# Strassen's products in an attention-and-MLP megakernel: one ScalarE copy out of PSUM with the sums on GpSimd, in place of two VectorE additions; small vectors loaded behind the first weights

## The chip, the cores and the metric

The kernel runs on one core of a Trainium2 chip, in float32 throughout. The metric is the device time of one launch in microseconds: 3781.12 us in the median of three runs (3780.70 to 3781.87).

A core has five engines that run side by side, each through its own queue in order: PE (TensorE, matmuls), DVE (VectorE), ACT (ScalarE), POOL (GpSimd) and SP (SyncE, which here only issues DMAs). They meet in two memories, SBUF and PSUM. Matmuls write PSUM, which has eight banks of 128 x 512 float32.

## The reference

Two layers are applied to x of shape (16, 256, 32, 32): 16 batches, 256 channels, 1024 tokens. Cut to what matters:

```python
# layer 0: attention, 4 heads of 64
qkv  = xs @ w_proj + b_proj
attn = softmax(einsum('bihd,bjhd->bijh', q, k) * 64**-0.5, axis=2)
x    = einsum('bijh,bjhd->bihd', attn, v).reshape(B, S, 256) @ w_out + b_out + xs
# layer 1: attention, 8 heads of 32, then an MLP, each behind a group norm of 32 groups
x = x + attention(group_norm(x, gn1_w, gn1_b), qkv_w, proj_w, proj_b, phys_bias)
h = group_norm(x, gn2_w, gn2_b)
h = gelu(einsum('oc,bchw->bohw', mlp_w1, h) + mlp_b1)          # 256 -> 1024
x = x + einsum('oc,bchw->bohw', mlp_w2, h) + mlp_b2            # 1024 -> 256
```

## The kernel before

**Tiling.** Channels lie on the 128 partitions, in two blocks `co` (0 and 1); the 1024 tokens of a batch lie on the free axis, in two halves `t` of `TB` = 512. So x of one batch is four blocks of 128 x 512, named (co, t), and the result is accumulated in place in the tile of x (three such tiles, `bufs=3`).

**The second MLP matrix by Strassen.** The product of w2 (two output blocks by two halves of the hidden axis) with the hidden activations `g` (two halves of the hidden axis by two halves of the tokens) is a 2 x 2 block product. It is done with Strassen's seven products instead of eight. The seven combinations of w2's quarters are made once at the start, on POOL (`sum_quarters`, L149 to L155). The combinations of `g` are made per batch on POOL, by `combine` (L852 to L858), four additions of 128 x 512 for each of five combinations; for the last batch, 15, they are made on DVE. `mlp` (L828) returns a list of 16 steps `hidden` (first matrix and Gelu) and a list of seven steps `outputs`, one for each product, in the order 2, 5, 3, 4, 1, 6, 7 (the list `products`, L862). A step of `outputs` is a call of `reduce` (L873): four products of 128 x 128 weights with 128 x 512 activations accumulate in a PSUM tile, and then the tile is added to, or subtracted from, the blocks of x that need it. Products 2, 5, 3, 4 and 1 go to two blocks each, products 6 and 7 to one. Each is one DVE instruction from PSUM (L889 with the bias `m2b`, L893 plus, L895 minus). The block whose last contribution this was is sent to memory by a DMA in SP's queue (L897).

**PSUM.** Three tiles of two banks each, "slots" 0 to 2 of the pool `ps_s`, and two single banks of `ps_a`. `wide` (L262) hands out the slot that was handed out longest ago. A step of `outputs` takes one slot, and a unit of scores in the second attention takes all three slots and both single banks. A tile can be written again once the instructions that read it are done.

**Order of the work.** The main loop (L965) goes over the 16 batches. One iteration b runs: the first attention of batch b (`attention_a`), with `later` holding delayed steps; the 16 hidden steps of batch b-1 (L981); the first projections of the second attention; and then the second attention of batch b (`attention_b`), 16 units of scores, each for two blocks of 128 keys. A generator's `yield` marks the end of a unit, and after each unit `run` (L907) inserts one or two other steps, from the dictionary `fill` (L993 to L1015). What is inserted is the rest of this layer's projections, then the seven products of batch b-1, alternating with pairs of projections for the first attention of batch b+1:

```python
for m, at_most in enumerate((1, 4, 6, 8, 10)):
    rest.insert(at_most, first[2 * m + 1 : 2 * m + 3])
```

So in iterations 1 to 14 a unit of scores follows a single product six times (2, 5, 3, 4, 1, 6), and a pair of projections in between. Iteration 0 has no products. In iteration 15 there is no next batch: products 2, 5 and 3 of batch 14 stand three units apart with nothing in between, 4, 1, 6 and 7 follow behind the attention (`end`, L1000), and then come the MLP steps of batch 15 (L1030). A program's order on each engine is the order in which these steps are issued; each engine waits by semaphores for what it needs.

**A unit of the second attention.** PE computes scores into the five PSUM tiles (`s_b`, L497); ACT takes exponentials out of them (`e_b`, L512); DVE sums exponentials (`es_b`, L527); PE weighs the values with the exponentials of the unit before (`acc_b`, L548); DVE adds that to the result (L561). Denominators (L570) are copied out by ACT (L323), travel through memory by SP's DMAs, are inverted by DVE (L332) and come back (L338) for a multiplication on DVE (L595). POOL also adds up the denominators and their inverses (L334, L335).

**Projections.** `qkv` (L725) has steps for q and k (emptied by ACT, L738 or L740) and for v (emptied by ACT, L759, in the first layer and by DVE, L761, in the second). Tiles q0, k0 and v0 of the next batch are made by `qkv_0` (L773).

**The start.** `load_wp` loads the projection weights of q (0), k (1) and v (2), half through ACT's queue and half through POOL's. Those of k are issued first. Then `load_vec` (L110) makes eight small vectors and issues the DMA of each in POOL's queue at once. `at_start` (L169) issues the weights of q and v and builds an identity matrix on POOL, which PE needs to transpose the bias of q and k (`bqk`, L936). `load_rest` (L159) issues the large weights in SP's queue.

Of the kernel before, what the change touches and what calls it, by code (L numbers as in the profile page):

```python
# [8 lines left out]
F32 = mybir.dt.float32  # L9
I32 = mybir.dt.int32  # L10
AF = mybir.ActivationFunctionType
ALU = mybir.AluOpType
AX = mybir.AxisListType

P = 128
GROUPS = 32
EPS = 1e-5
HEADS0, D0 = 4, 64
HEADS1, D1 = 8, 32
TB = 512  # L20
# [34 lines left out]
def kernel(  # L55
# [21 lines left out]
    nc = tc.nc  # L77
    B, C, S = x.shape
    HID = mlp_w1T.shape[1]
    CC = C // P  # L80
    SB = S // P
# [4 lines left out]
    const = ctx.enter_context(tc.tile_pool(name="const", bufs=1))  # L86
# [18 lines left out]
    mhalf = const.tile([P, CC], F32, name="mhalf")  # L105
    nc.gpsimd.memset(mhalf, -0.5)
    ones = const.tile([P, D0 // 2], F32, name="ones")
    nc.gpsimd.memset(ones, 1.0)

    def load_vec(v, n, name):  # L110
        t = const.tile([P, n], F32, name=name)
        nc.gpsimd.dma_start(t, v.rearrange("(c p) -> p c", p=P))
        return t

    bo = load_vec(b_out, CC, "bo")
    g1w = load_vec(gn1_w, CC, "g1w")
    g1b = load_vec(gn1_b, CC, "g1b")
# [4 lines left out]
    m2b = load_vec(mlp_b2, CC, "m2b")  # L122
# [15 lines left out]
    w2s = const.tile([P, 7, HID // P // 2, P], F32, name="w2s")  # L138
# [10 lines left out]
    def sum_quarters():  # L149
        q11, q22 = w2s[:, 2], w2s[:, 3]  # L150
        nc.gpsimd.tensor_sub(w2s[:, 5], w2s[:, 1], q11)
        nc.gpsimd.tensor_add(w2s[:, 1], w2s[:, 1], q22)
        nc.gpsimd.tensor_sub(w2s[:, 6], w2s[:, 4], q22)
        nc.gpsimd.tensor_add(w2s[:, 4], w2s[:, 4], q11)
        nc.gpsimd.tensor_add(w2s[:, 0], q11, q22)  # L155

    def load_rest():  # L159
        nc.scalar.dma_start(pb, phys_bias.partition_broadcast(P))  # L160
        for t, w in weights:
            nc.sync.dma_start(t, w)


    gavg = const.tile([P, P], F32, name="gavg")
# [29 lines left out]
    eones = const.tile([P, HEADS1, D1], F32, name="eones")  # L195
# [3 lines left out]
        nc.vector.tensor_copy(eones, ebias.unsqueeze(2).to_broadcast([P, HEADS1, D1]))  # L199

    bvo = const.tile([P, CC], F32, name="bvo")

    in_range = const.tile([P, 1], I32, name="in_range")

    with ExitStack() as first:
        first_pass(
            first, tc, x, out,
            dict(
                wp=wp, bqk=bqk, pb=pb, bo=bo, g1w=g1w, g1b=g1b, g2w=g2w,
                g2b=g2b, pjb=pjb, m1b=m1b, m2b=m2b, wo=wo, wq=wq, wpj=wpj, w1=w1,  # L210
                w2s=w2s, gavg=gavg, mhalf=mhalf, ones=ones, eones=eones,
                bvo=bvo, at_start=at_start, load_rest=load_rest, exp_bias=exp_bias,
                sum_quarters=sum_quarters,
                in_range=in_range,
            ),
        )
# [14 lines left out]
def first_pass(ctx, tc, x, out, k):  # L231
    nc = tc.nc
    B, C, S = x.shape
    CC, SB, NT = C // P, S // P, S // TB
# [3 lines left out]
    act = ctx.enter_context(tc.tile_pool(name="act", bufs=1))  # L238
# [483 lines left out]
        means()  # L722


    def qkv(key, D, src, weights, b_qk, v_scale, qT, kT, v_dst):  # L725
        def qk(ch, which, t):
            ps = single(f"qk_{key}_{ch}_{which}_{t}")
            for cc in range(CC):
                product(
                    ps,  # L730
                    weights(cc, which)[:, ch * P : (ch + 1) * P],
                    src[:, cc, t * TB : (t + 1) * TB],
                    start=(cc == 0),
                    stop=(cc == CC - 1),
                )
            d = (kT if which else qT)[:, ch, t * TB : (t + 1) * TB]
            if b_qk is None:
                nc.scalar.copy(d, ps)  # L738
            else:
                nc.scalar.activation(  # L740
                    d, ps, AF.Identity, bias=b_qk[:, which, ch : ch + 1]
                )

        def v(n):
            ps = single(f"v_{key}_{n}")
            for i in range(2):
                sb = 2 * n + i
                for cc in range(CC):
                    product(
                        ps[:, i * C : (i + 1) * C],  # L750
                        src[:, cc, sb * P : (sb + 1) * P],
                        weights(cc, 2),
                        start=(cc == 0),
                        stop=(cc == CC - 1),
                    )
            d = v_dst[:, 2 * n : 2 * n + 2]
            ps = ps.rearrange("p (b h d) -> p b h d", b=2, d=D)
            if v_scale is None:
                nc.scalar.copy(d, ps)  # L759
            else:  # L760
                nc.vector.tensor_mul(  # L761
                    d, ps, v_scale.unsqueeze(1).to_broadcast([P, 2, C // D, D])
                )

        return (
            [
                lambda ch=ch, which=which, t=t: qk(ch, which, t)
                for ch in range(CC) for which in (1, 0) for t in range(NT)
            ],
            [lambda n=n: v(n) for n in range(SB // 2)],  # L770
        )

    def qkv_0(b, xb):  # L773
        q = act.tile([P, CC, S], F32, tag="q0", name=f"q0_{b}")
        kk = act.tile([P, CC, S], F32, tag="k0", name=f"k0_{b}")
        v = act.tile([P, SB, HEADS0, D0], F32, tag="v0", name=f"v0_{b}")
        return (q, kk, v), qkv(
            f"a{b}", D0, xb,
            lambda cc, which: k["wp"][:, cc, which].rearrange("p h d -> p (h d)"),
            k["bqk"], None, q, kk, v,  # L780
        )

    def qkv_1(b, xn):
        q = act.tile([P, CC, S], F32, tag="q1", name=f"q1_{b}")
        kk = act.tile([P, CC, S], F32, tag="k1", name=f"k1_{b}")
        v = act.tile([P, SB, HEADS1, D1], F32, tag="v1", name=f"v1_{b}")
        return (q, kk, v), qkv(
            f"b{b}", D1, xn,
            lambda cc, which: k["wq"][:, cc, which * C : (which + 1) * C],
            None, k["eones"], q, kk, v,  # L790
        )

    def attention_0(b, qkv_tiles, xb, norm):
        q, kk, v = qkv_tiles
        stats = small.tile([P, CC, NT, 6], F32, tag="st0", name=f"st0_{b}", bufs=2)

        def project(t, res):
            return out_proj(
                f"o{b}", k["wo"],
                lambda kc: res[:, kc, t * TB : (t + 1) * TB],  # L800
                k["bvo"], xb, t, stats, (lambda: norm(stats)) if t == NT - 1 else None,
            )

        return attention_a(b, q, kk, v, project)

    def attention_1(b, qkv_tiles, xb, norm):
        q, kk, v = qkv_tiles
# [20 lines left out]
    def mlp(b, xb, hn):  # L828
        n4 = HC // 2
        gs = {}  # L830
        add_to = nc.gpsimd if b < B - 1 else nc.vector
# [20 lines left out]
        def combine(to, what, plus):  # L852
# [7 lines left out]


        products = [  # L862
            (2, (0, 0), [(1, 0, True, True), (1, 1, False, False)], ((0, 0), (1, 1))),
            (5, (1, 1), [(0, 1, True, True), (0, 0, False, False)], None),
            (3, (0, 1), [(0, 1, True, False), (1, 1, True, True)], ((0, 1), (0, 0))),
            (4, (1, 0), [(0, 0, True, True), (1, 0, True, False)], ((1, 0), (0, 0))),
            (1, (0, 0), [(0, 0, True, False), (1, 1, True, False)], None),
            (6, (0, 1), [(1, 1, True, False)], None),
            (7, (1, 0), [(0, 0, True, False)], None),
        ]  # L870
        missing = {(0, 0): 4, (0, 1): 2, (1, 0): 2, (1, 1): 4}

        def reduce(number, right, outs, then):  # L873
            ps = wide(f"m2_{b}_{number}")[:, 0, :]
            for i in range(n4):
                product(
                    ps, k["w2s"][:, number - 1, i], gs[(*right, i)],
                    start=(i == 0), stop=(i == n4 - 1),
                )
            for co, t, plus, bias in outs:  # L880
                missing[co, t] -= 1

                num = 2 if b == B - 1 and number == 7 else 1
                for u in range(num):
                    n = TB // num
                    sl = slice(t * TB + u * n, t * TB + (u + 1) * n)
                    y, p = xb[:, co, sl], ps[:, u * n : (u + 1) * n]
                    if bias:
                        nc.vector.scalar_tensor_tensor(  # L889
                            y, p, k["m2b"][:, co : co + 1], y, ALU.add, ALU.add  # L890
                        )
                    elif plus:
                        nc.vector.tensor_add(y, y, p)  # L893
                    else:
                        nc.vector.tensor_sub(y, y, p)  # L895
                    if not missing[co, t]:
                        nc.sync.dma_start(out[b, co * P : (co + 1) * P, sl], y)  # L897
            if then:
                combine(*then, True)
# [35 lines left out]
    ps, n = bank("bqk", 0), brow.shape[0]  # L935
# [399 lines left out]
```

## Time and profile before

| What | Value |
|---|---|
| Median of three runs | 3781.12 us (3780.70 to 3781.87) |
| Profiled execution, time and span | 3782.21 us, 3780.4 us |
| Mean granted TensorE clock | 0.998 |
| PE busy | 3751.6 us (99%) |
| DVE busy | 2459.8 us (65%) |
| ACT busy | 2036.6 us (54%) |
| POOL busy | 565.4 us (15%) |
| From one iteration to the next, iterations 1 to 14 | 233.45 us |
| First scores of the first attention | 34.08 us after the span's start |
| Score unit behind a product, from its start to that of acc_b: products 2, 5, 3, 4, 1, 6 | 2.65, 3.30, 3.17, 2.65, 2.64, 1.90 us |
| Additions of g on POOL (L855) | 300 of 1553 ns in the mean |

A line of the timeline gives the start, the time it took, the engine, the source line, the operation, what it writes and reads, the shape and the number of instructions; in brackets stands the idle time of the engine before it, and what ended it. A line of the waits gives who waited, for whom, the sum in us, how often, and the longest. The times of PE come from modelled ends, so a stretch of PE is best measured from the start of one group to the start of the next.

### The profile page before, as it was taken

To read this page: it belongs to the slowest core of one execution; us is meant where nothing else is said; L and a number is where in the kernel's file an instruction comes from. 1 tells how busy PE (TensorE), PEld (TensorE's weight loads), DVE (VectorE), ACT (ScalarE), POOL (GpSimd) and SP (SyncE) were. 2 spreads that over 40 slices of the span, in tenths; PEclk is the share of its full clock that TensorE was granted. 3 is DMA by queue.
4 is the path that set the end of the run, shared out by engine and by line. 5 is a ranking of instruction groups with operands and counts; after the bars stand their busy time and mean duration, and the time that the engine had idled before them with its cause. 6 is when DMAs were issued, how large, how long until landed. Compare 5 with 4: busy or idle time off the path is not lost.

```text
span 3780.4 us, 79539 instructions
## 1 busy us (share of the span) xinstructions
PE 3751.6 (99%) x34349; PEld 1329.2 (35%) x34349; DVE 2459.8 (65%) x2850; ACT 2036.6 (54%) x2624; POOL 565.4 (15%) x550
## 2 busy tenths in 40 slices
PE   9999999999999999999999999999999999999998
PEld 3333342333423334233342333333333333333323
DVE  4685657756576665766657666576665766657675
ACT  4565546555465554545546455554555546555462
POOL 1002112021120211202012020120201212011111
PEclk9999999999999999999999999999999999999999
DMA  2000100001001000010000101001010000100000
GB/s 85 10 16 10 33 12 13 30 10 33 12 13 35 7 30 13 19 30 7 30 13 19 29 7 34 9 19 30 8 34 7 23 25 13 30 7 23 14 8 26
DMA packets 63396, 77.80 MB, mean 21 GB/s; under 512 B 35038, under 2 KB 37854, under 8 KB 63038
## 3 DMA queue, kind: packets, MB, share of 16 engines
q1 hardware_dynamic: 60892, 71.85, 6.4%
q8 instruction: 271, 4.44, 0.5%
q10 hardware_dynamic: 1746, 0.40, 0.1%
q14 instruction: 87, 0.71, 0.1%
q0 software_dynamic: 400, 0.41, 0.1%
HBM read 54.28 MB, written 17.56 MB: 19 GB/s over the span
## 4 chain that ended last, share of the span: by engine, by line
PE 90%; DVE 4%; issue 3%; DMA 1%; ACT 1%; SPq 0%; POOL 0%; DVEq 0%; ACTq 0%; POOLq 0%
PE s_b L497 12%; PE m L836 12%; PE s_a L363 12%; PE acc_b L548 11%; PE acc_a L384 11%; PE m L309 7%; PE qk_b L309 6%; PE qk_a L309 5%; PE v_b L309 3%; PE o L309 3%; PE v_a L309 3%; PE j L309 3%; DVE es_b L527 2%; PE den_b L570 1%; PE den_a L415 1%
## 5 line engine op out<-in xcount | busy, mean ns | idle before, releaser
L512 ACT ACTIVATE e_b<-s_b 128x1024 f32<-128x1024 f32 (+1 forms) x1280 | 983.0, 864 | 394.2 <-PE s_b L497 394.2
L527 DVE TENSOR_TENSOR es_b<-es_b,e_b 128x1024 f32<-128x1024 f32 x768 | 961.5, 1300 | 258.2 <-ACT e_b L512 256.5
L371 ACT ACTIVATE e_a<-s_a 128x1024 f32<-128x1024 f32 x512 | 521.4, 1025 | 359.7 <-PE s_a L363 348.5
L497 PE MATMUL s_b<-q,k 32*64 32x512 f32 x8192 | 588.9, 603 | 14.9 <-DVE x L895 6.8
L855 POOL TENSOR_TENSOR g<-g,g 128x512 f32<-128x512 f32 x300 | 458.8, 1553 | 760.4 <-PE m L309 739.7
L363 PE MATMUL s_a<-q,k 64*64 64x512 f32 x4096 | 532.5, 593 | 1.1
L384 PE MATMUL acc_a<-e_a,v 64*64 64x512 f32 x4096 | 528.4, 589 | 0.0
L396 DVE TENSOR_TENSOR es_a<-es_a,e_a 128x1024 f32<-128x1024 f32 x384 | 469.3, 1222 | 74.7 <-ACT e_a L371 59.1
L548 PE MATMUL acc_b<-e_b,v 128*32 128x512 f32 x4096 | 494.6, 601 | 0.0
L836 PE MATMUL m<-gn_h,w 128*128 128x512 f32 x1024 | 452.8, 596 | 0.0
L309 PE MATMUL m<-g,w2s 128*32 128x512 f32 (+1 forms) x3320 | 404.2, 592 | 0.0
L844 ACT ACTIVATE g<-m,m1b 128x512 f32<-128x512 f32 x256 | 174.4, 687 | 288.7 <-PE m L836 288.5
L497 PEld LDWEIGHTS s_b<-q,k 32*64 32x64 f32 x8192 | 174.4, 130 | 395.5 <-issue 198.1
L836 PEld LDWEIGHTS m<-gn_h,w 128*128 128x128 f32 x1024 | 191.0, 190 | 235.9 <-issue 232.4
L384 PEld LDWEIGHTS acc_a<-e_a,v 64*64 64x64 f32 x4096 | 161.8, 133 | 277.7 <-issue 235.9
L363 PEld LDWEIGHTS s_a<-q,k 64*64 64x64 f32 x4096 | 152.4, 133 | 278.3 <-issue 208.0
L561 DVE TENSOR_TENSOR res_b<-res_b,acc_b 128x512 f32<-128x512 f32 x192 | 131.2, 683 | 181.6 <-PE acc_b L548 181.6
L309 PE MATMUL qk_a<-x,wp 128*32 128x512 f32 (+1 forms) x1856 | 236.1, 594 | 3.4 <-DMA wp<-in_L_conv_w_proj_dram 3.4
L548 PEld LDWEIGHTS acc_b<-e_b,v 128*32 128x32 f32 x4096 | 108.8, 109 | 359.4 <-ACT e_b L512 195.3
L309 PE MATMUL qk_b<-gn_g,wq 128*32 128x512 f32 (+1 forms) x1280 | 234.1, 592 | 0.0
L309 PEld LDWEIGHTS m<-g,w2s 128*32 128x32 f32 (+1 forms) x3320 | 122.2, 112 | 261.5 <-issue 246.6
L761 DVE TENSOR_TENSOR v<-v_b,eones 128x512 f32<-128x512 f32 x64 | 44.1, 688 | 201.8 <-PE v_b L309 201.8
(130 smaller groups left out, 2436.4 us busy)
## 6 DMA issues: line engine op xcount, KB each, us to landing
d_a<-row_a SPq DMA_DIRECT2D x64, 256.0 KB
rd_b<-row_b SPq DMA_DIRECT2D x252, 64.0 KB
out_dram<-x SPq DMA_DIRECT2D x63, 256.0 KB
x<-in_x_dram SPq DMA_DIRECT2D x30, 512.0 KB
x<-in_x_dram SPq DMA_DIRECT2D x4, 256.0 KB
w<-in_L_conv_mlp_w_dram SPq DMA_DIRECT2D x1, 1024.0 KB
w2s<-in_L_conv_mlp_w_dram SPq DMA_DIRECT2D x4, 256.0 KB
sp_b<-rd_b SPq DMA_DIRECT2D x63, 8.0 KB
```

Source lines behind the costliest of these rows:

```text
L309: nc.tensor.matmul(o[sl], w[:, sl], r, **flags)
L363: nc.tensor.matmul(s[h : h + HALF, g, :], kT[g * D : (g + 1) * D, c, kb * P + h : kb * P + h + HALF], qT[g * D : (g + 1) * D, c, t * TB : ...
L371: nc.scalar.activation(e, s, AF.Exp, scale=float(D) ** -0.5)
L384: nc.tensor.matmul(accs[i][h][g * D : (g + 1) * D, :], v[h * HALF : (h + 1) * HALF, kb, c * 2 + g], e[h * HALF : (h + 1) * HALF, g, :], st ...
L396: nc.vector.tensor_add(sums[i], held[i] if kb == 1 else sums[i], e)
L497: nc.tensor.matmul(outs[g][h : h + HALF, :], kT[g * D : (g + 1) * D, c, k0 : k0 + HALF], qT[g * D : (g + 1) * D, c, t * TB : (t + 1) * TB] ...
L512: nc.scalar.activation(to, s, AF.Exp, scale=float(D) ** -0.5)
L527: ins = nc.vector.tensor_add(d, es[n] if kb == 0 else d, es[2 * block + n])
L548: nc.tensor.matmul(acc[g * D : (g + 1) * D, :], v[:, kb + m, c * G + g], es[2 * m + g // 2][:, g % 2, :], start=(m == 0), stop=(m == 1),)
L836: nc.tensor.matmul(ps, k["w1"][:, cc, hc * P : (hc + 1) * P], hn[0][:, cc, t * TB : (t + 1) * TB], start=(cc == 0), stop=(cc == CC - 1),)
L844: nc.scalar.activation(g, ps, AF.Gelu, bias=k["m1b"][:, hc : hc + 1])
L855: ins = (add_to.tensor_add if plus else add_to.tensor_sub)(d, d, gs[(*what, i)])
```

## The change

Two parts.

First, the vectors. `load_vec` no longer issues its DMA; it puts it on a list, and `load_rest` issues the eight DMAs in POOL's queue, behind the weights of q and v and behind the identity matrix.

Second, the products. A product that goes to two blocks is read from PSUM by one ACT instruction into a quarter of an SBUF tile `lent`, 128 x 4 x 512, which takes the place of the next batch's v0 (so v0 is now made only when its first step runs). The two additions then read `lent` instead of PSUM, on POOL for batches 0 to 14 and on DVE for batch 15. Products 6 and 7 stay on DVE, from PSUM. The bias m2b goes in with the ACT instruction of products 2 and 5. Each of these is added to one block and subtracted from another, so the second block would miss two biases' worth; products 6 and 7 add twice m2b (`m2b2`) there. `combine` behind products 2, 3 and 4 stands behind the two additions in POOL's queue. The matmuls and SP's DMAs keep their order.

```diff
     def load_vec(v, n, name):
         t = const.tile([P, n], F32, name=name)
-        nc.gpsimd.dma_start(t, v.rearrange("(c p) -> p c", p=P))
+        vectors.append((t, v.rearrange("(c p) -> p c", p=P)))
         return t
...
         nc.gpsimd.tensor_add(w2s[:, 0], q11, q22)
+        nc.gpsimd.tensor_add(m2b2, m2b, m2b)
...
         for t, w in weights:
             nc.sync.dma_start(t, w)
+        for t, v in vectors:
+            nc.gpsimd.dma_start(t, v)
...
-            d = v_dst[:, 2 * n : 2 * n + 2]
+            d = v_dst()[:, 2 * n : 2 * n + 2]
...
-        v = act.tile([P, SB, HEADS0, D0], F32, tag="v0", name=f"v0_{b}")
+        made = []
+        def v():
+            if not made:
+                made.append(act.tile([P, SB, HEADS0, D0], F32, tag="v0", name=f"v0_{b}"))
+            return made[0]
...
-            for co, t, plus, bias in outs:
+            bias, num, add_to = None, 1, nc.vector
+            if len(outs) == 1:
+                bias = k["m2b2"]
+                num = 2 if b == B - 1 and number == 7 else 1
+            elif number in (2, 5):
+                bias = k["m2b"]
+            co = outs[0][0]
+            if len(outs) == 2:
+                if not lent:
+                    lent.append(act.tile([P, 4, TB], F32, tag="v0", name=f"lent_{b}"))
+                m = lent[0][:, number % 4]
+                if bias is not None:
+                    nc.scalar.activation(m, ps, AF.Identity, bias=bias[:, co : co + 1])
+                    bias = None
+                else:
+                    nc.scalar.copy(m, ps)
+                ps = m
+                if b < B - 1:
+                    add_to = nc.gpsimd
+            for co, t, plus in outs:
                 missing[co, t] -= 1
-                num = 2 if b == B - 1 and number == 7 else 1
+                n = TB // num
                 for u in range(num):
-                    n = TB // num
                     sl = slice(t * TB + u * n, t * TB + (u + 1) * n)
                     y, p = xb[:, co, sl], ps[:, u * n : (u + 1) * n]
-                    if bias:
+                    if bias is not None:
                         nc.vector.scalar_tensor_tensor(
-                            y, p, k["m2b"][:, co : co + 1], y, ALU.add, ALU.add
+                            y, p, bias[:, co : co + 1], y, ALU.add, ALU.add
                         )
-                    elif plus:
-                        nc.vector.tensor_add(y, y, p)
                     else:
-                        nc.vector.tensor_sub(y, y, p)
+                        (add_to.tensor_add if plus else add_to.tensor_sub)(y, y, p)
                     if not missing[co, t]:
                         nc.sync.dma_start(out[b, co * P : (co + 1) * P, sl], y)
```

## The prediction

> **What bounds the kernel now.** I read the page first. Its line for PE says 99% busy, so what PE does not idle away visibly must be found elsewhere. Then who waited for whom, PE only: barely 20 us in all.
>
> ```profile
> PE   3751.6 (99%) x34349; PEld 1329.2 (35%) x34349; DVE 2459.8 (65%) x2850; ACT 2036.6 (54%) x2624; POOL 565.4 (15%) x550
> ...
> PE s_b L497 <- DVE x L895: 6.8, 16, 1.7
> PE s_b L497 <- DVE res_b L561: 4.3, 5, 1.8
> PE qk_a L309 <- DMA wp<-in_L_conv_w_proj_dram: 3.4, 1, 3.4
> PE s_b L497 <- DVE x L889: 2.9, 14, 0.2
> ```
>
> Lines 889 and 895 are the second of the two VectorE additions that empty a Strassen product: scores wait for its PSUM. The page warns that ends of matmuls are modelled, so I took the third view, the timeline of PE, and measured from the start of one group to the start of the next (iteration 3, counted from 0, second attention):
>
> ```profile
> 829.32 2.72 PE L497 MATMUL s_b<-q,k 32*64 32x512 f32 x32
> 831.97 1.92 PE L548 MATMUL acc_b<-e_b,v 128*32 128x512 f32 x16
> 833.71 3.62 PE L309 MATMUL qk_a<-x,wp 128*32 128x512 f32 x32
> 837.26 1.97 PE L497 MATMUL s_b<-q,k 32*64 32x512 f32 x32
> 839.16 1.92 PE L548 MATMUL acc_b<-e_b,v 128*32 128x512 f32 x16
> 840.90 3.62 PE L309 MATMUL m<-g,w2s 128*32 128x512 f32 x32
> 844.45 1.95 PE L497 MATMUL s_b<-q,k 32*64 32x512 f32 x24
> 846.73 1.09 PE L497 MATMUL s_b<-q,k 32*64 32x512 f32 x8 [0.34 <-DVE x L895]
> 847.74 1.92 PE L548 MATMUL acc_b<-e_b,v 128*32 128x512 f32 x16
> ```
>
> The same 32 score matmuls take 837.26 to 839.16 = 1.90 us after a projection (qk_a) and 844.45 to 847.74 = 3.29 us after product 5. Only 0.34 of these 1.39 us is shown as a wait; the rest hides in overlapping modelled ends, as after product 2 (829.32 to 831.97 = 2.65). The cause stands on DVE and ACT:
>
> ```profile
> 837.39 0.69 ACT L740 ACTIVATE q<-qk_a,bqk 128x512 f32<-128x512 f32 x1 [1.03 <-PE qk_a L309]
> ...
> 845.24 0.75 DVE L889 SCALAR_TENSOR_TENSOR x<-m,m2b,x 128x512 f32<-128x512 f32 x1
> 845.90 0.68 DVE L895 TENSOR_TENSOR x<-x,m 128x512 f32<-128x512 f32 x1
> ```
>
> A unit of scores uses all three two-bank slots, the one last filled as its third, needed 0.9 us in. One ACT operation frees that slot 837.39+0.69-837.26 = 0.82 us after the scores begin, with no loss. Two DVE operations free it at 1.49 us when DVE is free (product 2: the second ends at 830.81, the scores began at 829.32), and at 845.90+0.68-844.45 = 2.13 us after product 5, where a normalising multiply stands ahead. Iterations 1 to 14 repeat these numbers to 0.01 us: 2.65, 3.30, 3.17, 2.65, 2.64 after products 2, 5, 3, 4, 1 and 1.90 after product 6, which has a single DVE addition.
>
> The start is the other loss:
>
> ```profile
> 7.46 0.73 POOL L112 DMA_DIRECT2D m2b<-in_L_conv_mlp_b_dram  x1
> ...
> 8.25 1.53 POOL L93 DMA_DIRECT2D wp<-in_L_conv_w_proj_dram  x2
> ...
> 15.12 12.12 PE L309 MATMUL qk_a<-x,wp 128*128 128x512 f32 x22 [3.43 <-DMA wp<-in_L_conv_w_proj_dram]
> ```
>
> The query weights stand in POOL's queue behind eight vectors. After the 3.43 us wait the window 15 to 20 us shows a granted clock of 0.50.
>
> **What the Trainium skill says.** "PSUM — Partial Sum Buffer", The four PSUM rules: GpSimd cannot touch PSUM, so the ACT copy is what lets POOL add at all. "SBUF — State Buffer", Who interferes with whom: a VectorE instruction with two SBUF inputs contends with a GpSimd instruction that reads SBUF; PE and ACT wait on nobody. The trace agrees: the sum of exponentials (L527) takes 1.22 us with POOL idle and 1.74 us in the mean (1.53 to 2.31) where POOL adds throughout. "ScalarE: Activation LUTs", Table sets: identity and copy are in every set; here L740 (Identity) runs among exponentials and the only loads are one per change between Exp and Gelu (31). "TensorE: Matmul & The Clock Gate", part 1: an idle window of about 3.4 us halves the clock; the 0.50 above agrees.
>
> **The change, part by part, against the span of 3780.4 us** (profiled execution 3782.21, median 3781.12; the median is 0.7 above the span).
>
> *Vectors behind the weights.* POOL loses 8 issues of 0.73 to 0.91 us (2.33 to 8.19) ahead of the two wp issues, which so start near 2.5 instead of 8.25. The first wp of that queue, issued at 1.30, landed at 6.80; the last two landed 1.9 and 1.2 us after their predecessors, so I estimate 8 to 9.5 us. PE needs them at about 11.1 and 20. The identity matrix on POOL (10.07 to 10.36) moves to about 5, so the 0.27 us of waiting for it goes too. From 10.16, PE then has 0.1 us of transpose, 24 matmuls at 0.429 us (the spacing of the 64 hidden matmuls, 27.47/64) and 6.84 us of v projections: scores begin at 27.4 instead of 34.08. **-6.6 us.** Bounds: -3.7 (the clock drops anyway) to -7. Behind the moved vectors on POOL stand the sums of w2 quarters, which start when w2s lands (20.13), while the vectors are issued by about 11; m2b2, one tiny addition, hides there. bo is read near 30 us, the others after 90; their DMAs took 3.6 to 5.7 us. x's second half shares the DMA engines with 256 KB more and is needed only near 13.7.
>
> *Products 2, 5, 3, 4, 1 of batches 0 to 13 (iterations 1 to 14).* Removed from DVE: two operations each, 7.0 us per batch. Added on ACT: one of 0.69 (Identity with bias, row L740) or 0.59 (copy, row L759), placed where ACT idles: before product 5's exponentials it waited 3.35 us for PE, and they begin at 845.57, 1.12 us after the scores do, while the copy ends at 0.82. So the projection case applies: 1.90. Saved per iteration 0.75+1.40+1.27+0.75+0.74 = 4.91, times 14 = **-68.7 us**. If ACT were not free the copy would cost what it removes.
>
> *Added on POOL:* ten additions per batch, SBUF to SBUF, price of row L855: 1.27 alone, 1.59 beside DVE, so 15.9 us. POOL is busy 22.6 of the 74.8 us from 825.8 to 900.6. Combining g after products 2, 3 and 4 moves behind two additions (3.2 us): 3.2+6.7 = 9.9 us after product 3, with about 19 us to product 4. DVE gains 7.0 and loses by contention 15.9 x (1.74-1.22)/1.74 = 4.8; it was busy 55.3 of those 74.8. The accumulator addition (L561) that frees PE's bank has some 2 us in hand, so I take 0; bounds 0 to +0.2 us for each of 70 products (+14), and no gain below 0, since 1.90 is the floor of every unit. The tile lent takes v's place: v's first eviction comes at about 893.6, the last POOL addition ends near 888.5. Output DMAs in SP's queue wait for POOL: product 3's goes from 854.4 to 855.4, and the next issue behind it is at 859.7.
>
> *Products 6 and 7* add 2 x m2b: 0.75 instead of 0.69 us on DVE. Slot freed at 0.88 instead of 0.82; where v_b is emptied by a late 0.69 us operation the trace has 1.97. +0.07 x 14 = **+1.0**.
>
> *Iteration 15* (products 2, 5, 3 of batch 14, other units without filling): product 2's 4.66 us, and the half clock behind it (acc_b 3.15, den_b 1.26), shrink until ACT binds: exponentials end at 3648.36, then the denominator copy, so the next scores start near 3649.1 instead of 3652.47, -3.4. After products 5 and 3 the exponentials ran back to back (3.83 for 5), so ACT paces and little comes: -0.2. POOL's longer queue after product 3 stretches DVE: +0.6. **-3**, bounds -7 and +1.
>
> *End:* product 7's two half additions carry a bias, +0.1. Products 4 and 1 put four additions into POOL before the power for the last norm (3718.81): about +0.2. Batch 15's additions stay on DVE, behind a copy, under 24 us of matmuls. **+0.3.**
>
> Sum: -6.6-68.7+1.0-3.0+0.3 = -77.0; span 3703.4, predicted 3704.1.
>
> **Rivals.** (1) *Contention gives back a third to a half*: POOL's additions slow DVE so that L561 is late. For: single pairs of L527 took 4.5 us beside POOL. Against: the 2 us in hand. 0.4 us per product is 70 x 0.4 = 28: 3732. (2) *The change doesn't free the scores*, because something else holds them at the same moment: only the start is left, 3774. Against: the 1.90 after projections and product 6. (3) *Slower*: product 6 adds on DVE to a block that product 1's POOL addition must have finished; DVE stands there in order, with L527 and L561 behind it. POOL has about 12 us in hand (888.5 against 900.7). From product 2's end (829.4) POOL has 22 operations before that block is ready; it comes too late once they take (900.7-829.4)/22 = 3.2 us each, and the iteration loses more than its 4.8 us gain from 3.5 us on. At 3.6 us it loses 22 x 0.4 = 8.8: 3781 + 14 x (8.8-4.8) - 9 = 3828. The longest L855 seen is 2.29, the mean beside DVE 1.59.
>
> **How the numbers follow.** Forecast 0.72 (its own range 3694 to 3718: start ±2, contention 0 to 14, iteration 15 ±4), rival 1 0.17 (3718 to 3755), rival 2 0.05 (3755 to 3774), no change 0.02, rival 3 0.03; 0.01 is a gain beyond the forecast. Eight in ten: 3693 to 3724, the upper end into rival 1. 0.2% (7.6 us) is about what a measurement of this kernel tells from no change: faster 0.95, same 0.02, slower 0.03.
>
> **What would show it.** PE's waits on x L889/L895 gone; 32 scores after every product 1.90; iterations 228.6 us apart instead of 233.45; no wait for wp, scores from 27.4 us; L527's mean up from 1300 to 1350 to 1420 ns; POOL some 810 us busy. I am wrong if scores stay over 2.5 us after a product, if L561 or POOL appears as PE's releaser in iterations 1 to 14, or if DVE waits for POOL's x.

## The result, and the profile after

The changed kernel takes **3763.81 us** in the median (3763.14 to 3765.74, five runs) against 3781.12 of the kernel before beside it (five runs). The ratio is 0.9954, with a 95% interval of 0.9940 to 0.9969. It is faster, but by 17.3 us where 77 were forecast.

The profiled spans go from 3780.4 to 3762.0 us, 18.4 less. I split both at the first hidden-layer matmul of the MLP of batch 0, and at the same place 14 iterations on:

| Part | Before | After | Difference | Forecast |
|---|---|---|---|---|
| Start, up to the first hidden matmul | 287.10 | 280.58 | -6.5 | -6.6 |
| Iterations 1 to 14, each | 233.45 | 232.15 | -1.30, 14 times -18.2 | -4.84, 14 times -67.7 |
| Iteration 15 and the end | 224.99 | 231.30 | +6.3 | -2.7 |

The start came as forecast. The page's line of busy times and the waits of PE show what took the place of the old waits:

```profile
PE 3699.7 (98%) x34349; PEld 1327.1 (35%) x34349; DVE 2563.5 (68%) x2700; ACT 2085.8 (55%) x2704; POOL 904.7 (24%) x701
```

```profile
PE s_b L502 <- DVE res_b L566: 47.0, 48, 3.1
PE gm_h L314 <- DVE mean_c_h L689: 3.4, 1, 3.4
```

The waits of scores for the additions to x (formerly L889 and L895) are gone. In their place stand 47.0 us of waiting for L566, the addition of a unit's result to the accumulator (L561 before), which frees one of the two single banks. VectorE has 150 instructions fewer and is busy 104 us longer.

The timeline of PE, iteration 3, around products 5, 3 and 1 (start, duration, line, what it writes and reads, and in brackets the idle time and what ended it):

```profile
831.04 3.62 PE L314 MATMUL m<-g,w2s 128*32 128x512 f32 x32
835.40 1.98 PE L502 MATMUL s_b<-q,k 32*64 32x512 f32 x32 [0.75 <-DVE res_b L566]
837.31 1.92 PE L553 MATMUL acc_b<-e_b,v 128*32 128x512 f32 x16
839.05 3.62 PE L314 MATMUL m<-g,w2s 128*32 128x512 f32 x32
843.32 1.98 PE L502 MATMUL s_b<-q,k 32*64 32x512 f32 x32 [0.65 <-DVE res_b L566]
...
869.39 3.62 PE L314 MATMUL m<-g,w2s 128*32 128x512 f32 x32
874.40 1.98 PE L502 MATMUL s_b<-q,k 32*64 32x512 f32 x32 [1.39 <-DVE res_b L566]
876.30 1.92 PE L553 MATMUL acc_b<-e_b,v 128*32 128x512 f32 x16
```

From the start of the scores to acc_b it is 835.40 to 837.31 = 1.91 us after product 5 (3.30 before), and 1.90 after product 1 (2.64 before): this is what the change was forecast to do. But products 5, 3 and 1, ahead of them, now last 4.36, 4.27 and 5.01 us from start to start, where a product without a wait lasts 3.55: 0.81 + 0.72 + 1.46 = 3.0 us lost per iteration. Another 0.46 us go behind product 1's unit: from its acc_b to the next scores it is 6.62 us, where it was 6.16 before. Of the 4.75 us that the six units of scores gained, 1.3 are left.

Why L566 is late can be read on VectorE and GpSimd, at the same time:

```profile
822.44 8.92 DVE L532 TENSOR_TENSOR es_b<-es_b,e_b 128x1024 f32<-128x1024 f32 x4 [3.44 <-ACT e_b L517]
...
831.45 3.30 DVE L532 TENSOR_TENSOR es_b<-es_b,e_b 128x1024 f32<-128x1024 f32 x2
834.67 0.67 DVE L566 TENSOR_TENSOR res_b<-res_b,acc_b 128x512 f32<-128x512 f32 x1
```

```profile
821.11 2.51 POOL L929 TENSOR_TENSOR x<-x,lent 128x512 f32<-128x512 f32 x2 [1.24 <-ACT lent L911]
823.58 8.93 POOL L868 TENSOR_TENSOR g<-g,g 128x512 f32<-128x512 f32 x4
```

From 823.58 on the two engines run side by side and both crawl: four sums of exponentials in 8.92 us, four additions of g in 8.93, 2.23 us each. Alone, a pair of such sums takes 2.35 us (1.22 for one), and two additions took 2.51 us at 821.11. So beside additions a sum takes nearly as long as a sum and an addition one after the other. L566, one of whose inputs is in PSUM, takes its usual 0.67 us; it is only late. The groups say it for the whole run (busy time and mean in ns, then idle time before). First the kernel before, then the changed one:

```profile
L527 DVE TENSOR_TENSOR es_b<-es_b,e_b 128x1024 f32<-128x1024 f32 x768 | 961.5, 1300 | 258.2 <-ACT e_b L512 256.5
L855 POOL TENSOR_TENSOR g<-g,g 128x512 f32<-128x512 f32 x300 | 458.8, 1553 | 760.4 <-PE m L309 739.7
```

```profile
L532 DVE TENSOR_TENSOR es_b<-es_b,e_b 128x1024 f32<-128x1024 f32 x768 | 1100.7, 1480 | 249.5 <-ACT e_b L517 249.4
L868 POOL TENSOR_TENSOR g<-g,g 128x512 f32<-128x512 f32 x300 | 514.1, 1738 | 20.8 <-ACT g L857 20.8
L929 POOL TENSOR_TENSOR x<-x,lent 128x512 f32<-128x512 f32 x150 | 268.7, 1811 | 152.6 <-ACT lent L914 96.0 <-ACT lent L911 56.5
```

The sums' mean rose from 1300 to 1480 ns (1350 to 1420 forecast), that of the old additions of g from 1553 to 1738.

At the end of the kernel, VectorE, GpSimd and PE in one stretch of the timeline:

```profile
3686.13 3.70 POOL L868 TENSOR_TENSOR g<-g,g 128x512 f32<-128x512 f32 x3
3689.79 0.19 POOL L590 TENSOR_TENSOR isum<-isum,part 128x1 f32<-128x1 f32 x1
...
3690.01 0.17 DVE L1070 TENSOR_REDUCE top<-isum 128x1 f32<-128x16 f32 x1 [3.03 <-POOL isum L590]
...
3694.12 0.38 PE L314 MATMUL gm_h<-mean_c_h,gavg 128*128 128x2 f32 x2 [3.38 <-DVE mean_c_h L689]
```

VectorE's range check of the denominators (L1070) waits 3.03 us for a tiny GpSimd sum, which now stands behind the two additions and three of the four combinations of product 4. Behind the check on VectorE wait the last projection's eviction and the norm's statistics, and PE waits 3.38 us for these. In the kernel before it waited 0.5 us at this place:

```profile
PE gm_h L309 <- DVE mean_c_h L684: 0.5, 1, 0.5
```

In the changed kernel, the clock granted behind this wait, from 3694.2 to 3700, is 0.71.

### The profile page after: what moved, and what is told of

It is laid out like the page before. It is cut to its first block, busy times and chain, and to the rows that moved or that the text cites. A ratio compares the mean times of both kernels' runs of the same rounds, so it can differ in the third digit from the quotient of the medians.

```text
span 3762.0 us, 79474 instructions
## 1 busy us (share of the span) xinstructions
PE 3699.7 (98%) x34349; PEld 1327.1 (35%) x34349; DVE 2563.5 (68%) x2700; ACT 2085.8 (55%) x2704; POOL 904.7 (24%) x701
## 4 chain that ended last, share of the span: by engine, by line
PE 85%; issue 7%; DVE 5%; DMA 2%; ACT 1%; SPq 0%; ACTq 0%; POOL 0%; DVEq 0%
PE m L849 12%; PE s_a L368 12%; PE acc_a L389 11%; PE s_b L502 11%; PE acc_b L553 9%; PE m L314 6%; PE qk_b L314 6%; PE qk_a L314 4%; PE v_a L314 3%; PE v_b L314 3%; PE o L314 3%; PE j L314 3%; DVE es_b L532 3%; PE den_b L575 1%; DMA rd_b<-row_b 1%
## 5 line engine op out<-in xcount | busy, mean ns | idle before, releaser
L532 DVE TENSOR_TENSOR es_b<-es_b,e_b 128x1024 f32<-128x1024 f32 x768 | 1100.7, 1480 | 249.5 <-ACT e_b L517 249.4
L376 ACT ACTIVATE e_a<-s_a 128x1024 f32<-128x1024 f32 x512 | 521.0, 1024 | 360.1 <-PE s_a L368 348.4
L502 PE MATMUL s_b<-q,k 32*64 32x512 f32 x8192 | 530.1, 604 | 47.9 <-DVE res_b L566 47.0
L868 POOL TENSOR_TENSOR g<-g,g 128x512 f32<-128x512 f32 x300 | 514.1, 1738 | 20.8 <-ACT g L857 20.8
L339 POOL TENSOR_TENSOR dsum<-dsum,sp_b 128x16 f32<-128x16 f32 x63 | 45.0, 715 | 1150.5 <-DMA sp_b<-rd_b 1150.5
L929 POOL TENSOR_TENSOR x<-x,lent 128x512 f32<-128x512 f32 x150 | 268.7, 1811 | 152.6 <-ACT lent L914 96.0
L502 PEld LDWEIGHTS s_b<-q,k 32*64 32x64 f32 x8192 | 164.7, 131 | 381.3 <-issue 166.3
```

The costliest lines, as they stand in the source:

```text
L376: nc.scalar.activation(e, s, AF.Exp, scale=float(D) ** -0.5)
L502: nc.tensor.matmul(outs[g][h : h + HALF, :], kT[g * D : (g + 1) * D, c, k0 : k0 + HALF], qT[g * D : (g + 1) * D, c, t * TB : (t + 1) * TB] ...
L532: ins = nc.vector.tensor_add(d, es[n] if kb == 0 else d, es[2 * block + n])
L868: ins = (add_to.tensor_add if plus else add_to.tensor_sub)(d, d, gs[(*what, i)])
L929: (add_to.tensor_add if plus else add_to.tensor_sub)(y, y, p)
```

## The experiments

All are compared with runs of the kernel before on the same chip (3780.8 to 3781.4 us in the median). "Period" is the time from one iteration to the next, iterations 1 to 14; "the rest" is iteration 15 and the end. Line numbers after an edit can be shifted by a few from those of the changed kernel. The main question is the first table's middle row: do the 3.5 us per iteration that are missing come from contention between GpSimd and VectorE, or from something else in the new way of the products?

**The parts alone.** First the kernel before with the vectors moved; then the changed kernel with the vectors loaded at once:

```diff
     def load_vec(v, n, name):
         t = const.tile([P, n], F32, name=name)
-        vectors.append((t, v.rearrange("(c p) -> p c", p=P)))
+        nc.gpsimd.dma_start(t, v.rearrange("(c p) -> p c", p=P))
```

> The kernel before with only the vectors loaded behind the weights. If the two parts of the change add up: 3781.1 - 6.5 = 3774.6 us, scores from 27.6 us on, iterations still 233.45 us apart. If the start's gain is partly due to the second part: over 3776.

> The changed kernel with the vectors loaded at once as before. If the parts add up: 3763.8 + 6.5 = 3770.3 us, iterations 232.15 us apart. If they do not add up: away from that by over 2 us.

Vectors alone: 3774.55 us, ratio 0.9982 (0.9975 to 0.9989), period 233.45, first scores at 27.19 us instead of 34.08. Products alone: 3770.06 us, ratio 0.9971 (0.9960 to 0.9981), period 232.16. The gains of 6.8 and 11.3 us add up to 18.1; both together gave 17.3. The difference of 0.8 us is less than the runs of one kernel differ, so nothing shows that the parts disturb each other, and the shortfall is in the products.

**The additions on VectorE, still behind the ACT copy.** GpSimd keeps the combining of g:

```diff
                     nc.scalar.copy(m, ps)
                 ps = m
-                if b < B - 1:
-                    add_to = nc.gpsimd
```

> The changed kernel with the two additions of each product on VectorE for all batches, from the SBUF copy that ScalarE makes. Theory A (what the freed PSUM slots gained, 4.8 us per iteration, was given back because additions on GpSimd and sums of exponentials on VectorE exclude each other, and the accumulator addition then comes late): scores 1.90 us after each product, no waits of PE for L566 in iterations 1 to 14, iterations 228.6 us apart, 3703 to 3708 us. Rival B (VectorE has too much in front of the accumulator addition as soon as units follow each other faster, whoever adds): waits for L566 stay, iterations 231 us or more, 3740 us or more. Rival C (ScalarE's copy itself delays): same as B, with ScalarE as releaser.

Measured 3727.03 us, ratio 0.9858 (0.9842 to 0.9875), period 230.26, the rest 221.45: 36.8 us better than the change, and between the two expectations. The ACT copy is thus not what costs. PE's only stall in an iteration is 1.53 us, after the projections that follow product 4. VectorE and GpSimd behind product 4:

```profile
853.70 2.94 DVE L927 TENSOR_TENSOR x<-x,lent 128x512 f32<-128x512 f32 x2 [0.91 <-ACT lent L914]
856.55 4.53 DVE L532 TENSOR_TENSOR es_b<-es_b,e_b 128x1024 f32<-128x1024 f32 x2
861.00 0.67 DVE L566 TENSOR_TENSOR res_b<-res_b,acc_b 128x512 f32<-128x512 f32 x1
...
853.11 6.89 POOL L868 TENSOR_TENSOR g<-g,g 128x512 f32<-128x512 f32 x4
```

The combining, which was there before, now meets additions of VectorE from SBUF (2.94 us for two; the two from PSUM took 0.75 and 0.68) and then two sums (2.27 each). Even work that was not moved has become dearer.

This kernel tells one thing more. Nothing stands ahead of the combining in GpSimd's queue here, so behind product 2 it begins as early as in the kernel before, 1.2 us after the product's first matmul:

```profile
812.59 3.62 PE L314 MATMUL m<-g,w2s 128*32 128x512 f32 x32
...
813.80 5.19 POOL L868 TENSOR_TENSOR g<-g,g 128x512 f32<-128x512 f32 x3 [39.32 <-PE m L314]
```

And the sums of exponentials (L532) last 1318 ns in the mean over the whole run, close to the 1300 of the kernel before and far from the 1480 of the changed one.

**GpSimd writes but does not add.** Each GpSimd addition is replaced by a one-column copy and two fills of the block, so the result lacks these products:

```diff
+                    elif add_to is nc.gpsimd:
+                        nc.gpsimd.tensor_copy(y[:, :1], p[:, :1])
+                        for _ in range(2):
+                            nc.gpsimd.memset(y, 0.0)
```

> The changed kernel in which GpSimd does not add (the contribution of products 2, 5, 3, 4 and 1 is left out for batches 0 to 14): for each addition it reads one column of the copy and then fills the block twice with zeros, about 1.2 us of GpSimd that reads nothing from SBUF but that column. Theory A in its narrow form (what excludes VectorE is GpSimd's reading): sums of exponentials beside these fills take 1.22 us, the mean of L532 falls from 1480 to below 1300 ns, iterations 228.6 us apart, about 3705 us. Rival D (any GpSimd work on SBUF beside VectorE, or a late GpSimd queue, costs the same): mean 1400 or more, iterations 231 to 232 us, about 3760 us.

A single run took 3708.76 us, with a period of 229.07. The mean of the sums is 1348 ns, above the 1300 expected, and the trace shows why:

```profile
829.26 1.77 POOL L929 COPY x<-lent 128x1 f32<-128x1 f32 x2 [2.83 <-ACT lent L911]
830.96 1.92 POOL L931 MEMSET x<- 128x512 f32 x4
...
838.54 6.96 POOL L868 TENSOR_TENSOR g<-g,g 128x512 f32<-128x512 f32 x4
...
830.90 2.35 DVE L532 TENSOR_TENSOR es_b<-es_b,e_b 128x1024 f32<-128x1024 f32 x2
...
840.06 4.32 DVE L532 TENSOR_TENSOR es_b<-e_b,e_b 128x1024 f32<-128x1024 f32 x2
```

The four fills run wholly beside a pair of sums, and the pair keeps its 2.35 us. Beside the combining, 8 us later, a pair takes 4.32. Even the tiny copies take turns: 1.77 us for two while VectorE ends a sum and a multiplication, 0.30 where VectorE is idle (836.41). In this run, GpSimd instructions that only write cost VectorE nothing; those that read do.

**Nothing on GpSimd behind the products.** The third experiment, with the combining behind products 2, 3 and 4 on VectorE too:

```diff
-                ins = (add_to.tensor_add if plus else add_to.tensor_sub)(
+                on = nc.vector if plus else add_to
+                ins = (on.tensor_add if plus else on.tensor_sub)(
```

> The kernel with the additions of the products on VectorE (the run before this one), in which the sums of g behind products 2, 3 and 4 go to VectorE too, so that GpSimd adds nothing during the second attention. Theory A (GpSimd and VectorE exclude each other): L532 falls to 1.22 us in the mean, the wait for L566 of 1.5 us per iteration behind product 4 goes, iterations 228.5 to 229.5 us apart, 3700 to 3712 us. Rival B (VectorE has too much to do in order): its 2.6 us bursts in front of the accumulator addition bring waits for L566 after products 2, 3 and 4, iterations over 230.3 us, slower than 3727 us.

Measured **3704.41 us** (3702.49 to 3705.03), ratio 0.9799 (0.9782 to 0.9815), period 228.82, the rest 216.26. It beats both kernels. VectorE has 22 more instructions per iteration than in the changed kernel, and its sums, and PE's waits for L566, are:

```profile
L532 DVE TENSOR_TENSOR es_b<-es_b,e_b 128x1024 f32<-128x1024 f32 x768 | 899.7, 1219 | 199.4 <-ACT e_b L517 198.6
```

```profile
PE s_b L502 <- DVE res_b L566: 6.2, 7, 2.6
```

**GpSimd's instructions cut in halves.** If the engines take turns, instruction by instruction, a sum should wait for half as much when each GpSimd addition covers 256 columns:

```diff
-                        (add_to.tensor_add if plus else add_to.tensor_sub)(y, y, p)
+                        for h in range(0, TB, TB // 2):
+                            c = slice(h, h + TB // 2)
+                            (add_to.tensor_add if plus else add_to.tensor_sub)(
+                                y[:, c], y[:, c], p[:, c]
+                            )
```

and the same in `combine`.

> The changed kernel with every addition of GpSimd beside the second attention (to x, and of g) cut into two of 256 columns: the same work in twice as many instructions. Theory A as turn-taking (a VectorE sum waits out one GpSimd instruction, 1.07 us, and then runs): a sum beside GpSimd takes about 1.75 us in place of 2.29, the waits for L566 (2.8 us per iteration) shrink by half or more, 3735 to 3752 us. If VectorE loses by the amount of GpSimd work and not by turns: 2.29 stays in sum over more instructions, no gain or a loss by GpSimd's added overhead, 3760 to 3785 us.

Measured 3730.28 us, ratio 0.9866 (0.9850 to 0.9883), period 229.87, the rest 229.7: better than expected. Wholly beside GpSimd, a sum lasts 1.75 us in the median, not 2.29. Above 1.22 that is 0.53 instead of 1.07: half. The work is the same; only the length of a turn differs. The waits for L566 in iterations 1 to 14 are gone. The price is on GpSimd, whose pairs of halves now take longer than one whole, and a new wait of ACT comes of it:

```profile
871.67 4.75 POOL L933 TENSOR_TENSOR x<-x,lent 128x256 f32<-128x256 f32 x4
...
876.46 0.59 ACT L765 COPY v<-v_a 128x512 f32<-128x512 f32 x1 [2.33 <-POOL x L933]
```

The first copy of v waits until product 1's additions are done with the lent tile, whose memory it takes: the unit of scores behind it lasts 3.09 us instead of 1.90. The prediction named this memory and had 5 us in hand for it; with halves it is used up.

**Batch 14 on VectorE.** The changed kernel with `b < B - 2` in place of `b < B - 1`, for the last row of the first table:

> The changed kernel with the additions of batch 14, whose products run in iteration 15 and behind it, on VectorE. If the last stretch is 6.1 us longer since VectorE's range check stands in front of the last norm and waits for GpSimd's sum of inverses, which stands behind product 4's additions: 3763.8 - 6 = 3758 us, and no wait of 3.4 us for mean_c_h. If something else lengthened it: 3763 us.

Measured 3754.8 us, ratio 0.9931 (0.9915 to 0.9948); period 232.15 as in the changed kernel, the rest 221.46 instead of 231.30. Of these 9.8 us, 3.1 are in iteration 15's attention and 6.7 behind it; PE's wait for mean_c_h is not there. So the loss at the end comes from batch 14's additions on GpSimd; that it runs through the sum of inverses is read from the waits above.

**The combining moved in the kernel before.** Is the gain of the fifth kernel that of moving the combining alone? The same edit in `combine`, made in the kernel before, whose products still leave PSUM by two VectorE additions:

> The kernel before, with one edit: the combining of g behind products 2, 3 and 4 is done by VectorE instead of GpSimd. The products still leave PSUM by two VectorE additions, and the vectors are loaded as before. It tells whether the gain of moving the combining (22.6 us from the third to the fifth kernel of the experiments) is there on its own. Theory: no. The third score slot is still freed by two VectorE operations, so the 4.9 us per iteration stay, and VectorE gets 12 operations of 0.68 us more against about 4 us less stretching; 3775 to 3800 us, period 233 to 234.5. Rival, that contention alone set the time and the ScalarE copy is not needed: about 3758 us or less, period 231.9 or less.

Measured 3767.83 us, ratio 0.9963 (0.9949 to 0.9977), period 232.93. It gains 13.6 us, which I had not expected, but far less than the rival said. Only about half of it comes from the 14 iterations (0.5 us each); iteration 15 and the end take 217.3 us instead of 225.0. Score units after products 2, 5, 3, 4, 1 last 2.65, 3.30, 2.65, 2.65, 2.64 us: only product 3's has changed (3.17 before). The third slot is still freed late, as here behind product 5:

```profile
844.07 1.95 PE L497 MATMUL s_b<-q,k 32*64 32x512 f32 x24
846.35 1.09 PE L497 MATMUL s_b<-q,k 32*64 32x512 f32 x8 [0.34 <-DVE x L896]
847.37 1.92 PE L548 MATMUL acc_b<-e_b,v 128*32 128x512 f32 x16
...
844.87 0.74 DVE L890 SCALAR_TENSOR_TENSOR x<-m,m2b,x 128x512 f32<-128x512 f32 x1
845.53 0.68 DVE L896 TENSOR_TENSOR x<-x,m 128x512 f32<-128x512 f32 x1
```

The ACT copy is needed for the slots. To use nearly all that it gives, the combining has to leave GpSimd; halves used a good part of it with the combining left there.

**The change's own GpSimd additions, without the combining.** The changed kernel with that same edit in `combine` and nothing else:

> The changed kernel with the combining behind products 2, 3 and 4 on VectorE, while GpSimd keeps the ten additions per iteration that the change gives it. Theory, a price of 1.07 us of VectorE per GpSimd addition wherever it comes from: VectorE is busy about as long as in the changed kernel, but behind products 3 and 4 it is late by 2 x 1.07 + 4 x 0.68 = 4.9 us instead of 6 x 1.07 = 6.4, so that the waits for the accumulator addition shrink without going: 3712 to 3740 us, sums of exponentials 1280 to 1350 ns in the mean. Rival, that only the long runs of combining on GpSimd hurt and the change's own additions are free: 3704 us as with all additions on VectorE, and the sums at 1220 to 1250 ns.

Measured **3705.76 us** (3705.11 to 3707.84), ratio 0.9801 (0.9785 to 0.9817), period 228.80. The time is the rival's, and cannot be told from that of the fifth kernel: my theory of one price for every addition fell. In the profiled executions the iterations are equal, and the rest is 219.44 us, 3.2 more than in the fifth kernel. The rival is right on the time, but not on its reason. GpSimd's additions are not free. VectorE beside GpSimd behind product 3:

```profile
834.50 2.35 DVE L532 TENSOR_TENSOR es_b<-es_b,e_b 128x1024 f32<-128x1024 f32 x2
836.77 4.66 DVE L869 TENSOR_TENSOR g<-g,g 128x512 f32<-128x512 f32 x4
841.35 0.68 DVE L566 TENSOR_TENSOR res_b<-res_b,acc_b 128x512 f32<-128x512 f32 x1
...
836.40 3.27 POOL L930 TENSOR_TENSOR x<-x,lent 128x512 f32<-128x512 f32 x2 [4.64 <-ACT lent L915]
```

Two GpSimd additions meet four short VectorE additions, which take 4.66 us instead of 2.49; two turns are lost, and then it is over. L566 ends at about 842.0, and PE wants its bank only at 843.58.

The busy time of VectorE from product 2 to the scores behind product 6 gives the price of a GpSimd addition in each kernel. VectorE's own work is taken from the two kernels that have none on GpSimd there: 58.07 us with the ACT copy (in it, five pairs of additions to x at 1.29 us and three times four of g at 2.49, which the others give to GpSimd in whole or in part), 58.40 without it (with three times 2.49).

| Kernel | GpSimd additions | VectorE busy | its own | lost | per addition |
|---|---|---|---|---|---|
| Before | 12 of g | 55.35 | 58.40 - 7.5 = 50.9 | 4.4 | 0.37 |
| Changed | 12 of g, 10 to x | 62.66 | 58.07 - 7.5 - 6.4 = 44.2 | 18.5 | 0.84 |
| Additions on VectorE | 12 of g | 61.10 | 58.07 - 7.5 = 50.6 | 10.5 | 0.88 |
| Only additions on GpSimd | 10 to x | 58.21 | 58.07 - 6.4 = 51.7 | 6.5 | 0.65 |
| In halves | 24 and 20 halves | 55.69 | 44.2 | 11.5 | 0.52 a pair |

A full turn costs 1.07 us. How near an addition comes to it depends on what VectorE does at that moment. In the kernel with the additions on VectorE (0.88), half of the 10.5 us lies on these additions themselves: the ten are busy for 11.54 us, against 6.47 in the fifth kernel. In the kernel before they read PSUM and kept their time.

## Why the prediction was right and wrong

**Right: the start.** -6.5 for -6.6 us. The weights landed at 7.07 and 7.66 us, before the 8 to 9.5 that I estimated, scores began at 27.58 instead of 27.4.

**Right: the slots.** The units of scores behind the five two-block products last 1.90 or 1.91 us in all 14 iterations, as forecast from the unit behind a projection. The unit behind product 6 lasts 2.03, 0.13 more for the 0.07 forecast. The copy is on ACT in time. The last experiment, with the combining off GpSimd, has the forecast's period (228.80 us for 228.6) and no stall of PE in an iteration. That its span of 3703.7 us also meets the 3703.4 of the sum is in part luck: the start, the iterations and the rest gained 6.1, 65.1 and 5.5 us where 6.6, 67.7 and 2.7 were forecast.

**Wrong: the step "loses by contention 15.9 x (1.74-1.22)/1.74 = 4.8", and from it "I take 0" for L561.** Contention rose by 14.1 us per iteration (18.5 - 4.4 in the table), three times as much, and VectorE's busy time in the stretch did not fall by 2.2 but rose by 7.3 us. Two things were wrong in that step. The mean of 1.74 is too low for a sum that meets additions from its start to its end: in the changed kernel such a sum lasts 2.29 = 1.22 + 1.07 us, and in the kernel before the 45 sums that lie wholly inside a run of GpSimd additions have a median of 2.30 already. And I priced only the ten new additions, leaving the twelve old ones at what they cost before, 0.37. (The ten also took GpSimd 1.81 us each, not 1.59.) Here is why the old ones were cheap, from the timeline of the kernel before, product 2, whose matmuls begin at 825.77:

```profile
826.99 4.73 POOL L855 TENSOR_TENSOR g<-g,g 128x512 f32<-128x512 f32 x3 [39.32 <-PE m L309]
...
825.77 2.35 DVE L527 TENSOR_TENSOR es_b<-e_b,e_b 128x1024 f32<-128x1024 f32 x2
829.46 0.75 DVE L889 SCALAR_TENSOR_TENSOR x<-m,m2b,x 128x512 f32<-128x512 f32 x1 [1.33 <-PE m L309]
830.13 0.68 DVE L895 TENSOR_TENSOR x<-x,m 128x512 f32<-128x512 f32 x1
831.56 4.62 DVE L527 TENSOR_TENSOR es_b<-es_b,e_b 128x1024 f32<-128x1024 f32 x3 [0.76 <-ACT e_b L512]
```

The combining began 1.2 us after the product's first matmul, and three of four additions passed while VectorE ended a pair of sums, idled and emptied PSUM. In the changed kernel, the product begins at 816.66 and the combining at 823.58, 6.9 us into it: it has to wait for the product's end, the copy and two additions. The next four sums begin at 822.44, so all four of its additions meet sums. I had written that the combining "moves behind two additions (3.2 us)" and asked only whether it would be in time for product 4. It moved by 5.7 us, from a gap onto the sums. The third kernel of the experiments supports this: there the combining begins early again, without the ten additions on GpSimd, and the sums' mean is 1318 ns.

The "2 us in hand" of L561 were there: behind product 5 it ended at 842.45 in the kernel before, and the scores began at 844.45. But four sums that take 8.92 us instead of 4.63 (as at 885.15) use up twice that. In the changed kernel L566 ends at 835.34 and the scores begin at 835.40, where 834.59 would have been possible. In all, the late sums and L566 cost PE 3.0 us of waits per iteration, and 0.46 more behind product 1's unit. I had bounded this loss at 14 us; the iterations lost 49.5 (67.7 - 18.2). The sign I had set for being wrong, L561 as PE's releaser in iterations 1 to 14, is what the waits show.

The Trainium skill's page "SBUF — State Buffer", Who interferes with whom, states who contends: a VectorE instruction with two SBUF inputs with a GpSimd instruction that reads SBUF. The runs agree on every side of it: the sums are stretched, L566 with one input in PSUM is not (0.67 us), and GpSimd's fills do no harm (2.35 for the pair beside them). How much a meeting costs was mine to measure in the trace before, and I took a mean for it.

**Wrong: iteration 15,** -3 forecast and +0.2 measured in its attention, by the same failed step: two units without filling wait 3.07 and 2.49 us for L566. With batch 14's additions on VectorE it is 138.47 instead of 141.61 us, the 3 us forecast.

**Wrong: the end,** +0.3 forecast and +6.1 measured. I followed GpSimd's queue to the power of the last norm, but not to the tiny sum of inverse denominators in front of it, for which VectorE's range check waits, with the norm's statistics behind it.

**The rivals.** Rival 1 had the right mechanism, contention makes L561 late, and too small a size: it gave back three quarters of the iterations' gain, not a third to a half. Rival 2 fell with the 1.90 us. Rival 3 did not come about: GpSimd's additions took 1.74 and 1.81 us in the mean, far from 3.2. But GpSimd's queue did cost at the end, at a place that no rival named.

What stays open: how much of the 18.5 us comes from the late start of the combining was not varied by itself. The third kernel starts it early with the ACT copy in place, but it also takes the ten additions off GpSimd; no run has both the early start and the ten additions there. And product 6's 0.06 us beyond the forecast go with a short wait of its VectorE addition for GpSimd's sum of inverses, which the timeline shows and no run took away alone.

## What to carry to other kernels

Before work goes to an engine that shares a memory path with another, price it by the worst meeting in the trace (here a sum between two additions), not by the mean; reprice the work that is already there, since taking away what covered it changes what it meets; and hold the sum against the slack of the one waiting instruction behind it. Where an addition can read one operand from PSUM, it escapes. If a shared path must be used, short instructions spread over the time cost less than long runs: without the combining behind them, the same ten additions left the time of an iteration as it was (228.80 and 228.82 us), and halves gained 33.5 us in all. And follow a queue that gets longer to every instruction in it, the tiny ones too.

## What was not expected of the hardware

- In these runs VectorE and GpSimd take turns, whole instructions at a time, when both have two SBUF inputs: a sum of 128 x 1024 lasts 1.22 us alone, 2.29 beside additions of 128 x 512, 1.75 beside additions of 128 x 256. An addition of 128 x 512 on GpSimd goes from 1.26 to 2.23 us at the same time.
- GpSimd fills of 128 x 512 (0.48 us each) leave the sums as they are, while a GpSimd copy of a single column waits for a sum to end: 1.77 us for two, 0.30 without.
- An addition of VectorE with one input in PSUM (0.67 us) keeps its time beside GpSimd; two with both inputs in SBUF went from 1.29 to 2.94 us.
